# VectorE's background work dealt out by one count in a decoder layer, and down weights loaded later

## The chip, the cores and the metric

The kernel runs on one core of a Trainium2 chip. The metric is the device time of one execution in microseconds (us), median of several runs. The engines are called PE (TensorE, matmuls; its weight loads run beside it as PEld), DVE (VectorE), ACT (ScalarE), POOL (GpSimd) and SP (SyncE, which issues the DMAs).

## The reference

One decoder layer on `x` (2 batches x 512 tokens x 1024), with a LayerNorm behind each of three blocks. Cut to what matters:

```python
q, k, v = x @ wq.T, x @ wk.T, x @ wv.T             # 32 heads of q, 8 of k and v, of 128
s = where(0 <= i - j < 128, q @ k.T / sqrt(128), -inf)   # 4 heads of q share one of k and v
x = layernorm(x + (softmax(s) @ v) @ wo.T)
fq = lambda t: (clip(round(t / s + z), 0, 255) - z) * s  # 8-bit fake quantisation
x = layernorm(x + fq(x) @ fq(ctx))                 # ctx: 1024 x 1024 for each batch
h = x / 128
act = int8(trunc(clip(silu(h @ w_gate.T) * (h @ w_up.T) * 128, -128, 127)))   # 2752 wide
x = layernorm(x + int8(trunc(clip(act @ w_down.T * 128, -128, 127))))
```

The ternary weights `w_gate`, `w_up` and `w_down` come as float32.

## The kernel before

The large products of the attention (projections of q, k and v, and the output product) and of gate and up run in float32 by Strassen's scheme in Winograd's form: a product of two by two blocks is made of seven products of blocks, which PE does as matmuls of 128 x 128 by 128 x 256, and of sums of blocks before and behind, which DVE does. `strassen_right_steps` makes the four sums `t` of the tokens' side (L102 to L108, each over 1024 values a partition), `strassen_left` the four sums `s` of the weights' side (L118 to L121, 512 values), and `strassen` the seven products and the sums of their results (`st`, `vT`, `kT`, `qT`, L147 to L178).

**Attention.** There are 16 groups `m`, (batch b, key head g), each of four token tiles i. While a group's scores, softmax and products with v are worked on (`scores`, `weigh`), `pieces(m + 1)` runs the three projections of the next group ahead, one of 21 steps at a time, and then `transpose_v` (tile `vtr`, L308). At the fifth step (k == 4) of a projection, `prepare` makes the sums L118 to L121 of a later one. The two batches have right sums of their own: `t_1` of batch 1 is made when group 7 of batch 0 starts (m + 1 == NKV, L437).

**Work behind, beside and ahead.** The function `other` is called six times in a tile, 24 times in a group. Each call takes one step of `rest` (the pieces), one step of `keeping` and then calls `between`, which is `in_attention` (L1062). That function has three queues of generators, and takes one step of each `behind` and `aside` in every call, and one of `ahead` in every fourth call or so.
- `keeping` (`keep`, `left_sums`, L405 to L426): the result of two tiles is copied into `factors` (L400), DVE makes the left sums of the output product (L407 to L412: four of 256 values, and behind the second pair of tiles four of 896), and DMAs store them in DRAM as `kept`.
- `behind`: from batch 0, group 2 on, the quantised context (L607 to L617) and the output product of each batch, `project_out`: 56 products `y` (L555) from `ol` (loaded from `kept`, L476) and `or` (loaded `wo` and its sums, L483; sums `ot`, L495 to L500), each set of whose results `read` adds to the residual (L523 to L546). After `read` come `gap` bare yields: four for batch 0, two for batch 1.
- `aside`: `cross_tokens(0)`, the token tiles 2, 3, 0, 1 of batch 0 for the cross product, when `ahead` is empty: LayerNorm (L77 to L85), quantisation (L607 to L617), transposes `q` (L671) copied to `a1T` (L672), product `m` (L678), sums and LayerNorm (L679 to L680, L62 to L85), transposes `x2` (L687) copied to `x2T` (L688), and in the last group the right sums `t2_0` for the feed-forward.
- `ahead`: the sums of the weights of the output product and of gate and up (L1033 to L1036, L1055 to L1058), stored by DMA.

**Feed-forward.** `feed_forward` works through units (batch b, a slice of 128 of the 2752). For each unit it loads the down weights `wd` (`load_down`, L738) and then the next unit's `wgu` and `sgu` (L703 to L706). ACT and DVE split `wd` into `hi` (L757) and `lo` (L758) for the product `d` (L801). `wd` has one buffer.

Within a block of the program a scheduler sets the order of each engine's instructions, from the order in the program and from buffers; the queues above decide where a step stands in the program.

Of the kernel before, what the change touches and what calls it, by code (L numbers as in the profile page):

```python
# [19 lines left out]
B = 2  # L20
# [67 lines left out]
def strassen_right(nc, pool, x, name):  # L88


    steps = strassen_right_steps(nc, pool, x, name)
    for factors in steps:
        pass
    return factors


def strassen_right_steps(nc, pool, x, name):

    b11, b12, b21, b22 = (x[:, ts(k, KH), ts(n, NH)] for k in range(2) for n in range(2))
    t = pool.tile([P, 4, KH, NH], F32, tag="t", name=name)  # L100
    t1, t2, t3, t4 = (t[:, k] for k in range(4))
    nc.vector.tensor_tensor(t1, b12, b11, ALU.subtract)  # L102
    yield
    nc.vector.tensor_tensor(t2, b22, t1, ALU.subtract)
    yield
    nc.vector.tensor_tensor(t3, b22, b12, ALU.subtract)
    yield
    nc.vector.tensor_tensor(t4, b21, t2, ALU.subtract)  # L108
    yield b11, b21, b22, t4, t1, t2, t3


def strassen_left(nc, tc, pool, w, name):
# [66 lines left out]
    yield  # L179


class Background:


    def __init__(self):
# [6 lines left out]
    def step(self):  # L192
        while self.queue:
            item = self.queue[0]
            item[2] += 1
            if item[2] % item[1]:
                return
            try:
                next(item[0])
                return  # L200
            except StopIteration:
                self.queue.pop(0)

# [4 lines left out]


def attention(nc, tc, consts, xbuf, tpool, wpool, ps_p, ps_y, dram, kept, complete, between):  # L210

# [3 lines left out]
    with ExitStack() as ctx:  # L217
# [65 lines left out]
        def project(n):  # L283

            b, g, j = order[n]
            if j == 0:
                c1 = kT[b, g] = kvpool.tile([P, N], F32, tag="kT", name=f"kT_{n}")
                c2 = vT[b, g] = kvpool.tile([P, N], F32, tag="vT", name=f"vT_{n}", bufs=1)
            else:
                if j == 1:  # L290
                    qT[b, g] = qpool.tile([P, N // BLOCK, G, BLOCK], F32, tag="qT", name=f"qT_{b}_{g}")
                c1, c2 = (qT[b, g][:, :, 2 * j - 2 + h] for h in range(2))
            if n == 0:
                project_first((c1, c2))
                yield
                return
            outs = [c[:, ts(half, c.shape[1] // 2)] for c in (c1, c2) for half in range(2)]
            for k, _ in enumerate(strassen(nc, (ps_p, ps_y if b == 0 else ps_p), work, lefts.pop(n), right[b], outs, n)):
                if k == 4:
                    prepare(n + 1)  # L300
                elif k == 6:
                    load_weight(n + 2)
                yield

        def transpose_v(b, g):
            ps = ps_t.tile([P, TPB, P], F32, tag="t", name=f"vtr_{b}_{g}")
# [77 lines left out]
        def weigh(pending, meanwhile):  # L384


            if pending is None:
                meanwhile()
                return
            b, g, i, s = pending  # L390
            cur, both = transpose_p(b, g, i, s)
            meanwhile()
            ps = ps_t.tile([P, G, P], F32, tag="t", name=f"o_{b}_{g}_{i}")
            if i == 0:
                nc.tensor.matmul(ps, v[b, g][:, 0, :], cur, start=True, stop=True)  # L395
            else:
                nc.tensor.matmul(ps, v[b, g][:, i - 1, :], both, start=True, stop=False)  # L397
                nc.tensor.matmul(ps, vd[b, g][:, i - 1, :], cur, start=False, stop=True)  # L398
            half, place = divmod(i, 2)
            nc.scalar.copy(factors[:, 2 * half : 2 * half + 2, 2 * place : 2 * place + 2],  # L400
                           ps.rearrange("p (k j) t -> p k j t", k=2))
            if place:
                keeping.add(keep(b, g, half))
# [10 lines left out]
        def keep(b, g, half):  # L414


            own = slice(2 * half, 2 * half + 2)
            yield from left_sums(*(factors[:, own, k] for k in range(7)))
            yield
            if half:  # L420
                yield from left_sums(*(factors[:, k] for k in range(7)), True)
            for k in (3, 4, 5, 2, 6) if half else (0, 1):
                nc.sync.dma_start(out=kept[b][:, g, k], in_=factors[:, k])
            if half:
                complete.add((b, g, "kept"))
            yield  # L426
# [2 lines left out]

        for _ in pieces(0):  # L430
            pass
        pending = None
        for m, (b, g) in enumerate(groups):
            if m + 2 == NKV:
                x1 = load_x(1)
            if m + 1 == NKV:
                right[1] = strassen_right(nc, tpool, x1, "t_1")  # L437
            rest = pieces(m + 1) if m + 1 < len(groups) else iter(())
            for i in range(TPB):

                def other():
                    next(rest, None)
                    keeping.step()
                    between(b, g, i)

                s = scores(b, g, i, other)
                weigh(pending, other)
                pending = b, g, i, s
                for _ in range(STEPS - 2):
                    other()  # L450
            for _ in rest:
                pass
        weigh(pending, lambda: between(B - 1, NKV - 1, TPB))
        keeping.drain()


def project_out(nc, tc, b, xres, spaces, psum, kept, complete, wo_d, sums, x_d, gap):
# [90 lines left out]
    for n, (k, g) in enumerate(steps):  # L548
        while n + 2 < len(steps) and (b, steps[n + 2][1], "kept") not in complete:
            yield  # L550
        left, mine, sums_now = lefts.pop(n), factors.pop(n), following
        for part in (order[:4], order[4:]):
            for j in part:
                bank, half = places[j]
                nc.tensor.matmul(  # L555
                    banks[bank][:, half], left[:, SLOT[j]], mine[j],
                    start=grow[k][0] and g == 0 and half == 0, stop=g == LAST, skip_group_check=True,
                )
            if part[0] == order[0]:
                next(sums_now, None)  # L560
                yield
        following = right_sums(n + 1)
        next(following)
        load_right(n + 3)
        load_left(n + 2)
        yield
        if g == LAST:
            read(k)
            if k in (5, 3):
                complete.add((b, 1 if k == 5 else 0))  # L570
            for _ in range(gap):
                yield


class Cross:
# [134 lines left out]
def feed_forward(nc, tc, ident, xres, spill, x2T, xbuf, tpool, wpool, left, right, gate_up, wd_d, pools, stream, ps_y, out, between, finish_between):  # L710

    one_pool, raw_pool, b_work, ps_p = pools
    with ExitStack() as ctx:
# [176 lines left out]

        todo, since, ends, room_x = [], [], [], []
        for u, (b, m) in enumerate(units):
            load_down(u)
            load_unit(u + 1)
            if m == NCHUNK:
                if b == 0:
                    finish_between()
                    right[1] = strassen_right(nc, tpool, x2T[1], "t2_1")
                rest_unit(u, b)
            else:  # L900
                g, up = gate_up_tiles(u)
                outs = g[:, :NH], g[:, NH:], up[:, :NH], up[:, NH:]
                for k, _ in enumerate(strassen(nc, (ps_p, ps_y if b else ps_p), work, left.pop(u), right[b], outs, u)):
                    if k == (0 if m == 0 else 3):
                        for args in todo:
                            down(*args)
                        todo = []
                    between(k)
                    if k in (2, 5) and ends:
                        norm(*finish(*ends.pop(0)))  # L910
                activate(u, g, up)
            split(u)
            since.append(u)
            if u < held_from and (len(since) == (4 if b else 2) or u + 1 == held_from):
                assert not todo
                todo = [(since, i, e) for i in range(TPB) for e in range(2)]
                since = []
# [25 lines left out]
def decoder_layer(ctx, tc, x, xT, ctx_kv, wq, wk, wv, wo, s1, z1, s2, z2, wgu, wgu_rest, wd, out):  # L943
# [50 lines left out]
    wo_sums = scratch.tile([P, 4, NKV, 2, HALF], F32, tag="wo_sums", name="wo_sums")  # L994

    def output(b):
        return project_out(nc, tc, b, xres, (resid, stream), ps_y, kept[b], complete, wo, wo_sums, x, 2 if b else 4)

    def cross_tokens(b):
        while ahead.queue:  # L1000
# [4 lines left out]
        while b == 0 and not last_group[0]:  # L1005
            yield
        if b == 0:
            for factors in strassen_right_steps(nc, tpool, x2T[0], "t2_0"):
                yield
            right[0] = factors  # L1010

    def weights_room(n, names):

# [45 lines left out]
            nc.sync.dma_start(out=sums[m][:, 0:3, k : k + 2], in_=s)  # L1059
            nc.sync.dma_start(out=sums[m][:, 3, k : k + 2], in_=a21)  # L1060

    def in_attention(b, g, i):  # L1062
        calls[0] += 1
        place = calls[0] % 6
        if (b, g, i, place) == (0, 2, 0, 1):
# [3 lines left out]
        if (b, g, i, place) == (1, 0, 1, 1):  # L1069
            behind.add(output(0))  # L1070
            behind.add(output(1))
            aside.add(cross_tokens(0))
        behind.step()
        aside.step()
        if b and g == NKV - 1:
            last_group[0] = True
            if place == 0:
                prepare_feed_forward()
        if (place == 0 and (b or g or i)) or (place == 3 and i % 2):
            ahead.step()  # L1080

    left, right = {}, {}

# [3 lines left out]
            if u not in left:  # L1087
                left[u] = load_factors(nc, wpool, gate_up, u, u)

    calls, in_first, last_group = [0], [True], [False]  # L1090
    ahead.add(sum_output_weights())
    ahead.add(sum_weights())
    attention(nc, tc, (ident, mask_i, keep_cur), xbuf, tpool, wpool, pools[3], ps_y,
# [66 lines left out]
```

## Time and profile before

| what | us |
|---|---|
| median of 3 runs (1948.54, 1948.76, 1952.91) | 1948.76 |
| the profiled execution | 1950.62 |
| its span | 1948.9 |
| PE busy | 1891.6 (97%) |
| DVE busy | 1368.4 (70%) |
| ACT busy | 564.3 (29%) |
| PE waits for `vT` (L175) ahead of `vtr` | 13.4, 4 times |
| PE waits for `ol` ahead of `y` | 5.5, 3 times |

The span is the time from the first to the last instruction in the profile. A matmul of 128 x 256 in float32 takes 0.38 us by the profile, and the pitch from one to the next is 0.43 us. A busy share is an average over all stages; what a change is worth is read in the place where an engine waits. The mean clock granted to PE over the span was 0.99 of full speed, and it falls in a few short stretches to half.

### The profile page before, as it was taken

What the parts mean: (1) busy time and instruction counts of PE and PEld (TensorE: products, weight loads), DVE (VectorE), ACT (ScalarE), POOL (GpSimd) and SP (SyncE); (2) the same over time, 40 slices, a digit from 0 to 9 for tenths busy, and PEclk for the clock granted to TensorE, in tenths of its full rate; (3) what the DMA queues carried; (4) which work ended last, traced back from release to release, by engine and by line L of the source; (5) the groups of instructions that cost most, each with busy time, mean ns of one, the idle gap of its engine ahead of it and who ended that gap; (6) DMA issues with size and microseconds to landing.
All of it is one profiled execution on the core that took longest, in us unless ns stands there. A gap on an engine that the chain in (4) does not pass through costs nothing.

```text
span 1948.9 us, 24631 instructions
## 1 busy us (share of the span) xinstructions
PE 1891.6 (97%) x8658; PEld 1553.0 (80%) x8668; DVE 1368.4 (70%) x3010; ACT 564.3 (29%) x1571; POOL 13.7 (1%) x32
## 2 busy tenths in 40 slices
PE   9999999999999999999899999999999999999997
PEld 6888888878888888888676788888877778888885
DVE  4678888777667677767776776566768697554656
ACT  1333343323122221233433221111233255221224
POOL 0000000000000000000000000000000000000000
PEclk9999999999999999999899999999999999999999
DMA  8478787767698788764376765666653245543421
GB/s 302 158 269 286 271 288 265 257 240 265 228 312 296 249 299 285 231 220 170 126 275 226 246 226 203 208 219 219 219 189 119 82 155 196 184 167 124 147 92 43
DMA packets 183323, 416.87 MB, mean 214 GB/s; under 512 B 16672, under 2 KB 93728, under 8 KB 183200
## 3 DMA queue, kind: packets, MB, share of 16 engines
q1 hardware_dynamic: 181760, 412.94, 61.7%
q10 hardware_dynamic: 1440, 2.36, 0.3%
q8 instruction: 68, 1.11, 0.2%
q14 instruction: 55, 0.45, 0.1%
HBM read 318.77 MB, written 96.47 MB: 213 GB/s over the span
## 4 chain that ended last, share of the span: by engine, by line
PE 77%; DVE 12%; DMA 6%; ACT 3%; issue 2%; SPq 0%; DVEq 0%; ACTq 0%
PE prod L138 43%; PE y L555 14%; PE d L801 7%; DMA wd<-in_wd_dram 4%; PE ps L338 3%; PE o L397 2%; PE o L398 2%; PE m L678 1%; PE pt L374 1%; ACT s L362 1%; PE first L273 1%; PE o L395 1%; DVE lo L758 1%; DVE factors L408 1%; DMA sums<-sum 1%
## 5 line engine op out<-in xcount | busy, mean ns | idle before, releaser
L555 PE MATMUL y<-or,ol 128*128 128x256 f32 x896 | 248.8, 382 | 5.6 <-DMA ol<-kept 5.5
L555 PEld LDWEIGHTS y<-or,ol 128*128 128x128 f32 x896 | 169.7, 191 | 31.8 <-issue 4.8
L555 PE MATMUL y<-ot,ol 128*128 128x256 f32 x672 | 184.4, 383 | 3.9 <-DVE ot L496 2.6
L138 PE MATMUL prod<-xT,w 128*128 128x256 f32 x752 | 184.0, 382 | 0.0
L138 PE MATMUL prod<-t,w 128*128 128x256 f32 x752 | 177.7, 379 | 0.0
L138 PE MATMUL prod<-t,s 128*128 128x256 f32 x752 | 177.2, 380 | 0.5 <-ACT kT L158 0.5
L138 PE MATMUL prod<-x2T,wgu 128*128 128x256 f32 x672 | 161.0, 380 | 1.7 <-ACT st L147 1.7
L138 PEld LDWEIGHTS prod<-xT,w 128*128 128x128 f32 x752 | 140.2, 191 | 27.6 <-issue 10.6
L138 PEld LDWEIGHTS prod<-t,w 128*128 128x128 f32 x752 | 140.2, 190 | 24.4 <-issue 7.2
L138 PEld LDWEIGHTS prod<-t,s 128*128 128x128 f32 x752 | 140.0, 190 | 24.6 <-issue 5.7
L138 PE MATMUL prod<-t,wgu 128*128 128x256 f32 x672 | 157.4, 380 | 1.8 <-DVE st L150 1.6
L138 PE MATMUL prod<-t,sgu 128*128 128x256 f32 x672 | 157.2, 380 | 1.5 <-ACT u L795 0.8
L555 PEld LDWEIGHTS y<-ot,ol 128*128 128x128 f32 x672 | 126.0, 191 | 27.1 <-DVE ot L496 8.2
L138 PEld LDWEIGHTS prod<-x2T,wgu 128*128 128x128 f32 x672 | 127.6, 191 | 20.9 <-ACT st L147 2.5
L138 PEld LDWEIGHTS prod<-t,wgu 128*128 128x128 f32 x672 | 127.1, 190 | 21.1 <-DVE st L150 2.4
L138 PEld LDWEIGHTS prod<-t,sgu 128*128 128x128 f32 x672 | 126.9, 190 | 20.7 <-ACT x2T L688 1.6
L348 ACT COPY s<-ps 128x128 f32<-128x128 f32 x192 | 39.7, 233 | 246.6 <-PE ps L338 246.6
L362 ACT ACTIVATE s<-s,top 128x128 f32<-128x128 f32 x256 | 100.2, 393 | 33.0 <-DVE top L359 32.6
L801 PE MATMUL d<-hi,act 128*128 128x512 f32 x256 | 108.4, 424 | 0.9 <-DVE act L781 0.4
L801 PE MATMUL d<-lo,act 128*128 128x512 f32 x256 | 101.5, 397 | 0.0
L815 DVE TENSOR_TENSOR acc<-d,acc 128x512 f32<-128x512 f32 x104 | 71.4, 690 | 41.4 <-PE d L801 40.9
L161 DVE TENSOR_TENSOR st<-prod,st 128x256 f32<-128x256 f32 x89 | 37.6, 422 | 89.3 <-PE prod L138 89.2
(213 smaller groups left out, 3000.1 us busy)
## 6 DMA issues: line engine op xcount, KB each, us to landing
kept<-factors SPq DMA_DIRECT2D x112, 448.0 KB, 3.8
ol<-kept SPq DMA_DIRECT2D x112, 448.0 KB, 5.0
w<-in_wq_dram SPq DMA_DIRECT2D x64, 512.0 KB, 4.5
or<-wo_sums SPq DMA_DIRECT2D x64, 512.0 KB, 4.7
sgu<-sums SPq DMA_DIRECT2D x42, 768.0 KB, 5.7
or<-in_wo_dram SPq DMA_DIRECT2D x48, 512.0 KB, 4.7
wgu<-in_wgu_dram SPq DMA_DIRECT2D x42, 512.0 KB, 4.0
wd<-in_wd_dram SPq DMA_DIRECT2D x42, 512.0 KB, 4.5
```

Source lines behind the costliest of these rows:

```text
L138: nc.tensor.matmul(ps, left[k - 1][:, c, :], right[k - 1][:, c, :], start=start and c == 0, stop=c == KH - 1, skip_group_check=True)
L161: nc.vector.tensor_tensor(u3, two, p1, ALU.add)
L273: nc.tensor.matmul(ps[h][:, part], weights[0][:, h, c], x0[:, c, part], start=c == 0 and k == 0, stop=c == KC - 1, skip_group_check=True,)
L338: nc.tensor.matmul(ps[:, k, cut // BLOCK : G + 1].rearrange("p d w -> p (d w)"), qT[b, g][:, G * i + c].rearrange("p h w -> p (h w)"), kT[ ...
L348: nc.scalar.copy(s[:, c, c * BLOCK :], ps[:, k, : G - c].rearrange("p d w -> p (d w)"))
L362: nc.scalar.activation(s[:, h, :], s[:, h, :], AF.Exp, bias=top[:, h : h + 1], scale=QSCALE, accum_out=total[:, h : h + 1],)
L374: nc.tensor.transpose(ps[:, :, ts(c, BLOCK)], s[:, c, :], ident)
L397: nc.tensor.matmul(ps, v[b, g][:, i - 1, :], both, start=True, stop=False)
L398: nc.tensor.matmul(ps, vd[b, g][:, i - 1, :], cur, start=False, stop=True)
L555: nc.tensor.matmul(banks[bank][:, half], left[:, SLOT[j]], mine[j], start=grow[k][0] and g == 0 and half == 0, stop=g == LAST, skip_group_ ...
L801: nc.tensor.matmul(ps, act[:, ts(i, P)], half[:, ts(e, HALF)], start=start and k == 0, stop=stop and k == len(parts) - 1)
L815: nc.vector.tensor_tensor(acc[t][:, ts(e, HALF)], ps, acc[t][:, ts(e, HALF)], ALU.add)
```

## The change

`strassen_right_steps` gives back its result and four functions, one for each sum. For `t_1` the first two are called when the group starts, and each of the next calls of `other` makes one more. One count replaces the fixed places of the queues: each call of `in_attention` steps `behind`; if the call already had a large step (k == 4 of a projection, a right sum, or a `read` that is followed by `gap`) nothing more is done; else one step of `keeping`, if it has any; else, with a credit of four calls, one step of `ahead`; else one of `aside`. `keeping` is emptied before `factors` is written again, and a bare yield in `keep` stays only for the second half. `gap` is two for both batches. In the feed-forward the next unit's gate and up weights are loaded first, and the unit's down weights after its second product. The diff, cut to that:

```diff
 def strassen_right_steps(nc, pool, x, name):
...
-    nc.vector.tensor_tensor(t1, b12, b11, ALU.subtract)
-    yield
...
+    less = lambda *which: lambda: nc.vector.tensor_tensor(*which, ALU.subtract)
+    return (b11, b21, b22, t4, t1, t2, t3), (less(t1, b12, b11), less(t2, b22, t1), less(t3, b22, b12), less(t4, b21, t2))
...
+LUMP = "lump"
...
 class Background:
             try:
-                next(item[0])
-                return
+                return next(item[0])
...
 def attention(...):
                     prepare(n + 1)
...
-                yield
+                yield LUMP if k == 4 else None
...
+            keeping.drain()
             nc.scalar.copy(factors[...], ps.rearrange(...))
...
             yield from left_sums(*(factors[:, own, k] for k in range(7)))
-            yield
             if half:
+                yield
                 yield from left_sums(*(factors[:, k] for k in range(7)), True)
...
             if m + 1 == NKV:
-                right[1] = strassen_right(nc, tpool, x1, "t_1")
+                right[1], late = strassen_right_steps(nc, tpool, x1, "t_1")
+                late = list(late)
+                for _ in range(2):
+                    late.pop(0)()
...
                 def other():
-                    next(rest, None)
-                    keeping.step()
-                    between(b, g, i)
+                    lump = next(rest, None)
+                    if late:
+                        late.pop(0)()
+                        lump = LUMP
+                    between(b, g, i, lump, keeping)
...
 def project_out(...):
-            for _ in range(gap):
-                yield
+            for j in range(gap):
+                yield None if j else LUMP
...
 def feed_forward(...):
         for u, (b, m) in enumerate(units):
-            load_down(u)
             load_unit(u + 1)
+            if m == NCHUNK:
+                load_down(u)
...
+                    if k == 1:
+                        load_down(u)
                     between(k)
...
-        return project_out(..., 2 if b else 4)
+        return project_out(..., 2)
...
-            for factors in strassen_right_steps(nc, tpool, x2T[0], "t2_0"):
+            right[0], steps = strassen_right_steps(nc, tpool, x2T[0], "t2_0")
+            for step in steps:
+                step()
                 yield
...
-    def in_attention(b, g, i):
+    def in_attention(b, g, i, lump, keeping):
         calls[0] += 1
         place = calls[0] % 6
...
-        behind.step()
-        aside.step()
+        if behind.step():
+            lump = LUMP
+
+        credit[0] += 1
+        if lump:
+            pass
+        elif keeping.queue:
+            keeping.step()
+        elif credit[0] >= 4 and ahead.queue:
+            credit[0] -= 4
+            ahead.step()
+        else:
+            aside.step()
...
-        if (place == 0 and (b or g or i)) or (place == 3 and i % 2):
-            ahead.step()
```

More of the change, by code (lines that the diff above doesn't have):

```diff
@@ L88, in strassen_right @@
 def strassen_right(nc, pool, x, name):
-    steps = strassen_right_steps(nc, pool, x, name)
-    for factors in steps:
-        pass
+    factors, steps = strassen_right_steps(nc, pool, x, name)
+    for step in steps:
+        step()
     return factors
@@ L101, in strassen_right_steps @@
     t1, t2, t3, t4 = (t[:, k] for k in range(4))
-    nc.vector.tensor_tensor(t1, b12, b11, ALU.subtract)
-    yield
-    nc.vector.tensor_tensor(t2, b22, t1, ALU.subtract)
-    yield
-    nc.vector.tensor_tensor(t3, b22, b12, ALU.subtract)
-    yield
-    nc.vector.tensor_tensor(t4, b21, t2, ALU.subtract)
-    yield b11, b21, b22, t4, t1, t2, t3
+    less = lambda *which: lambda: nc.vector.tensor_tensor(*which, ALU.subtract)
+    return (b11, b21, b22, t4, t1, t2, t3), (less(t1, b12, b11), less(t2, b22, t1), less(t3, b22, b12), less(t4, b21, t2))
 def strassen_left(nc, tc, pool, w, name):
@@ L418, in keep @@
             yield from left_sums(*(factors[:, own, k] for k in range(7)))
-            yield
             if half:
+                yield
                 yield from left_sums(*(factors[:, k] for k in range(7)), True)
@@ L431, in attention @@
             pass
-        pending = None
+        pending, late = None, []
         for m, (b, g) in enumerate(groups):
@@ L452, in attention @@
                 pass
-        weigh(pending, lambda: between(B - 1, NKV - 1, TPB))
+        weigh(pending, lambda: between(B - 1, NKV - 1, TPB, None, keeping))
         keeping.drain()
@@ L570, in project_out @@
                 complete.add((b, 1 if k == 5 else 0))
-            for _ in range(gap):
-                yield
+            for j in range(gap):
+                yield None if j else LUMP
 class Cross:
@@ L996, in output @@
     def output(b):
-        return project_out(nc, tc, b, xres, (resid, stream), ps_y, kept[b], complete, wo, wo_sums, x, 2 if b else 4)
+        return project_out(nc, tc, b, xres, (resid, stream), ps_y, kept[b], complete, wo, wo_sums, x, 2)
     def cross_tokens(b):
@@ L1007, in cross_tokens @@
         if b == 0:
-            for factors in strassen_right_steps(nc, tpool, x2T[0], "t2_0"):
+            right[0], steps = strassen_right_steps(nc, tpool, x2T[0], "t2_0")
+            for step in steps:
+                step()
                 yield
-            right[0] = factors
     def weights_room(n, names):
@@ L1088, in prepare_feed_forward @@
                 left[u] = load_factors(nc, wpool, gate_up, u, u)
-    calls, in_first, last_group = [0], [True], [False]
+    calls, credit, in_first, last_group = [0], [0], [True], [False]
     ahead.add(sum_output_weights())
```

## The prediction

> **What bounds the kernel now.** I read the page first: who is busy, then the clock.
>
> ```profile
> PE 1891.6 (97%) x8658; PEld 1553.0 (80%) x8668; DVE 1368.4 (70%) x3010; ACT 564.3 (29%) x1571; POOL 13.7 (1%) x32
> ...
> PEclk9999999999999999999899999999999999999999
> ```
>
> TensorE (PE) is the bound: 1891.6 of 1948.9 us, and the change removes no matmul. It can only win what PE loses: 57.3 us of idle time, and half of any time in which PE runs at half clock. The single 8 in the clock line says that such time exists. The waits of PE, totalled, say what it idles for (columns: us in total, times, longest):
>
> ```profile
> PE vtr L308 <- DVE vT L175: 13.4, 4, 7.5
> PE y L555 <- DMA ol<-kept: 5.5, 3, 2.7
> ...
> PE pt L374 <- DVE s L368: 1.2, 1, 1.2
> ```
>
> The largest is the transpose of v (`vtr`) waiting for VectorE's (DVE's) last sum of v. The third view is a table of windows around the long waits (us; busy PE, PEld, DVE, ACT, POOL; granted clock; DMA share; GB/s):
>
> ```profile
> 392.00:418.00 26.00, 21.30 (x88) 16.30 (x87) 20.82 (x45) 8.09 (x32) 0.00 (x0) 0.87 0.69 242
> 940.00:960.00 20.00, 11.17 (x45) 6.65 (x45) 13.96 (x28) 6.52 (x20) 0.00 (x0) 0.66 0.46 168
> 1008.00:1045.00 37.00, 32.11 (x128) 23.10 (x127) 21.66 (x54) 12.17 (x51) 0.00 (x0) 0.91 0.58 210
> 1045.00:1080.00 35.00, 29.26 (x124) 23.52 (x124) 29.76 (x59) 10.56 (x14) 0.00 (x0) 0.97 0.88 317
> 1080.00:1430.00 350.00, 347.70 (x1578) 292.65 (x1579) 230.53 (x469) 61.34 (x97) 0.00 (x0) 1.00 0.63 217
> ```
>
> A window's loss is its length less PE's busy time, plus its length times (1 − clock). A, 392 to 418: 4.7 + 3.4 = 8.1 us. C, 940 to 960: 8.8 + 6.8 = 15.6. D1, 1008 to 1045: 4.9 + 3.3 = 8.2. D2, 1045 to 1080: 5.7 + 1.1 = 6.8. Together 38.7 us in 118 us; the 350 us behind them lose 2.3. So the change is decided in four places.
>
> **Place A: the two sums of `t_1` and what follows.** VectorE in order of time:
>
> ```profile
> 403.44 1.08 DVE L407 TENSOR_TENSOR factors<-factors 128x896 f32<-128x896 f32 x1
> 404.44 0.69 DVE L118 TENSOR_TENSOR s<-w 128x512 f32<-128x512 f32 x1
> 405.04 1.08 DVE L408 TENSOR_TENSOR factors<-factors 128x896 f32<-128x896 f32 x1
> ...
> 407.85 1.09 DVE L411 TENSOR_TENSOR factors<-factors 128x896 f32<-128x896 f32 x1
> 408.85 1.09 DVE L412 TENSOR_TENSOR factors<-factors 128x896 f32<-128x896 f32 x1
> 409.85 0.42 DVE L175 TENSOR_TENSOR vT<-prod,st 128x256 f32<-128x256 f32 x1
> ```
>
> Starts lie about 1.0 us apart for a big sum and 0.6 for a sum of the next weights (L118 to L121), so 4 x 1.0 + 4 x 0.6 = 6.4 us stand between the previous sum of v and L175. PE waits 4.24 us behind it. In the changed order, which a build shows without a run, L411 and L412 stand behind L175: 2.0 us leave, and the wait is 2.2 at most. The group's four sums of 1.22 us (L102 to L108) are now spread over 8 us of PE work, the last of them 2 us later than before, with three weight sums of 0.42 (L1056 to L1058) between and four fewer behind; adding rows in that order leaves a wait of 0.7 us. I take 0.7 to 2.2 and no half clock, since waits of 1.2 (462 us) and 1.9 us (1146 us) stand in the trace with none behind them. A then loses 0.7 to 2.2 instead of 8.1: saved 5.9 to 7.4, taken 6.7. If the clock still trips, 2.5.
>
> **Place C: batch 1, group 6.** The same transpose waits longest here:
>
> ```profile
> 949.71 0.87 PE L308 MATMUL vtr<-ident,vT 128*128 128x128 f32 x3 [7.53 <-DVE vT L175]
> ...
> 954.17 2.34 PE L678 MATMUL m<-a,a1T 128*128 128x512 bf16 x5 [1.30 <-ACT s L362]
> ```
>
> Between the sums of v at 938.41 and 949.13 VectorE takes three small and four big left sums, the four L118s and the LN and quantise steps of one token tile (L85 0.82, L607 0.82, L612 and L613 0.70 each): 10.7 us in a row, of which PE covers three. In the changed order the quantise steps are elsewhere, the next weights' four stand behind the transposes, and three big sums, 3.1 us, remain, of which the product between (4 matmuls, 0.43 us apart) covers 1.7. So 1 to 2.5 us remain, no half clock. The moved token steps need their own place; the nearest rows, PE's wait of 1.30 for L362 above and 0.3 to 0.7 for L679 and the like, give 2 us more. C loses 3 to 4.5 instead of 15.6: saved 11.1 to 12.6, taken 11. Floor: if the 2.0 us that A loses are all that goes, PE still waits 5.5 + 1.3 and the clock trips: saved 2.
>
> **Place D1: the last group.** Something is given back here. Background work is rationed: a step that carries a lump, or that has kept sums queued, leaves nothing for `aside` (the token tiles). So tile 1's LN, quantise and products move from group 6 into group 7, among tiles 2 and 3. Adding rows in the changed order from the mask multiply of group 6's last tile (L380) to tile 1's second LN (L85): 8 left sums 5.5, LN and quantise 8.3, the softmax pieces L352 to L368 4.9, two L380 1.2, other 0.8: 20.7 us of VectorE beside 15.2 of PE. So PE stands 5.5 us behind by the transposes of x2. In front of it the first `m` follows its transposes directly, with no other product between, so it waits for the copies L672, 2 x 1.0 plus a hand-over: 2.2 to 2.95, taken 2.6. With `o` behind `both` (1.46, its row in D1), `q` 0.7, `act` 1.2: 11.5 us. Before, PE lost 4.9 here and ran 6.8 us at half clock (3.3). With a like spell of half clock, 2.5: 14.0 us after against 8.2, so 5.8 us given back. Bounds: none of the VectorE backlog reaches PE: 6 + 0, a gain of 2; PE at half clock in proportion to C (6.8 lost on 8.8 idle): 11.5 + 8.9 = 20.4, 12 given back.
>
> [...]
>
> **Place D2: `ol` behind `wd`.** At 1075.44 and 1078.19 PE waits 2.69 and 0.88 us for `ol`, whose loads leave SP's queue at 1069.30 and 1072.34, around the loads of `wd` (1060.52 and 1072.99) and a unit's own loads; the DMA share is 0.88. The change puts `wd` two products later in its unit, here behind `ol`. What then comes late is `d` behind `act` (0.78 at most in the trace) and `lo` (L758, 1.22 us) behind the `wd` landing, 1.6 to 2.5. D2 saves 4.3 to 5.2 of 6.8; 1 if the two waits are for room in the ring. Taken 5.
>
> **The rest.** The order of PE's products is the same from unit 3 to unit 21. In units 24 to 32 one split stands a place later: the row "PE prod L138 <- DVE u L164", 4.3 us in five waits, may gain or lose 1. `output(0)`'s shorter gap lets each of its steps begin two calls earlier: the additions hide under PE where DVE is 70% busy; a wait more like "PE y L555 <- DVE ot L496", 2.6 us in two, costs 1.3. Smaller waits for L352 in batch 0: 0.7. I charge 2 in all. Instructions added or removed: none; only two of four `t_1` sums, the tokens and loads move.
>
> **Sum.** 6.7 + 11 − 5.8 + 5 − 2 = 14.9 us. The profiled execution took 1950.62 (span 1948.9 and 1.7 around it), 1.9 above the median of 1948.76. So 1950.6 − 14.9 = 1935.7 for that one and 1933.9 for the median; I say 1934.
>
> **Rivals.** *Slower (1957): the last group stays at half clock.* If D1's waits follow one another so closely that the clock does not return over the 28 us of PE work from tile 1's `q` to the end of attention, each of these us takes two: 28 lost, + 11.5, against 8.2: 31.3 given back, where A, C and D2 save 22.7: 1948.8 + 8.6 + 2 = 1959; at 90% of it 1956. It turns the sign from 29 us lost in D1 on, and is told from no change from 35 on. For it: the clock of 0.91 after waits of 1.2 us. Against: one 20-us window, with 8.8 us idle, still had 0.66.
> *Waits shrink, the clock trips all the same (1943).* A saves 2.5, C 5 (a wait of 4 us left with its trip of 6.8), D1 gives back 5.8, D2 saves 5, 2 for the rest: 4.7 to 6 gained, 1943 to 1944. For it: `t_1` still shares VectorE's queue with kept sums.
> *The order moves but the same items end last (1947 to 1950).* If `ol` waits for room and the waits of A and C become waits for other lumps of the same size, nothing is left but noise: 0 ± 2. Against: 2.0 us leave A's queue and 6 leave C's by the order itself.
> *D1 is free (1927).* PE's other work, output products of batch 1, absorbs the backlog: − 5.8 becomes + 1.
>
> **How the numbers follow.** Forecast (1928 to 1942) 0.53; free D1 (1925 to 1928) 0.12; clock trips (1942 to 1946) 0.17; no change 0.07; half clock throughout 0.11. No difference under 0.3%, 5.8 us, can be told from none: faster is below 1942.9, slower above 1954.6. Faster: 0.53 + 0.12 + 0.13 of the third = 0.78; same: 0.04 + 0.07 + 0.01 = 0.12; slower: the other 0.10. A range of 1925 to 1948 leaves out the last case and small ends.
>
> **What would show it.** Right: no `vtr` behind L175 above 2.5 us, clock 0.97 or more over 392 to 418 and 1.00 over 930 to 960; more waits of `m`, `pt`, `ps` and `x2` between 1000 and 1040; no `y` behind `ol` above 1 us near 1075. Wrong: a clock under 0.8 over the last group, or vT waiting behind `t_1`.

## The result and the profile after

The changed kernel takes 1932.49 us (median of four runs, 1928.50 to 1933.06), the kernel before 1950.72 beside it; the ratio is 0.9902, 95% interval 0.9882 to 0.9922. The forecast was 1934, 0.8% less than before; 1.0% less is what came. The profiled execution took 1932.87 with a span of 1931.1, 17.8 us shorter than before. A line of the kernel before has another number now: L138 is L132, L175 is L169, L407 to L412 are L406 to L411, L118 to L121 are L112 to L115, L496 and L500 are L501 and L505, L555 is L560, L672 is L677, L678 is L683, L687 is L692, L801 is L806.

The page of the changed kernel, engine totals and clock:

```profile
PE 1886.3 (98%) x8668; PEld 1550.9 (80%) x8668; DVE 1367.3 (71%) x3010; ACT 563.0 (29%) x1571; POOL 13.7 (1%) x32
...
PEclk9999999999999999999989999999999999999999
```

The same work of VectorE, 1 us less, lies elsewhere; PE's idle time fell from 57.3 to 44.8 us. The 8 in the clock line has moved one slice on, from C to the last group. PE's waits, totalled:

```profile
PE prod L132 <- DVE u L158: 6.4, 6, 1.8
PE y L560 <- DVE ot L501: 4.9, 6, 2.1
...
PE ps L336 <- DVE s L350: 2.8, 2, 2.6
...
PE m L683 <- ACT a1T L677: 1.6, 2, 1.4
...
PE x L692 <- DVE xres L85: 1.5, 1, 1.5
...
PE vtr L306 <- DVE vT L169: 1.3, 1, 1.3
```

`vtr` behind `vT` fell from 13.4 us to 1.3, and `y` behind `ol` (5.5) is gone from the list. New are `ps` and `x`, and `m` rose from 0.2; all three stand among tile 1's steps in the last group. Windows of equal length cut the two executions at different work, since the second runs ahead; so the stretches are cut here where PE has the same amount of work behind it. The kernel before, stretches A, C, D1, D2 (start:end, length, then busy PE, PEld, DVE, ACT, POOL, granted clock, DMA share, GB/s):

```profile
387.70:430.50 42.80, 38.07 (x169) 30.13 (x168) 32.29 (x70) 12.22 (x49) 0.00 (x0) 0.92 0.69 237
929.30:966.90 37.60, 28.77 (x127) 21.24 (x127) 28.10 (x68) 15.69 (x44) 0.00 (x0) 0.82 0.36 128
991.00:1047.90 56.90, 51.62 (x223) 38.60 (x222) 39.54 (x90) 22.61 (x83) 0.00 (x0) 0.94 0.67 245
1047.90:1108.80 60.90, 55.16 (x237) 44.59 (x236) 45.24 (x90) 15.40 (x20) 0.00 (x0) 0.97 0.76 267
```

The changed kernel, the same four:

```profile
387.00:423.90 36.90, 35.49 (x168) 28.55 (x168) 31.95 (x70) 12.22 (x49) 0.00 (x0) 1.00 0.78 263
923.80:948.50 24.70, 24.66 (x126) 19.73 (x126) 19.36 (x47) 17.04 (x45) 0.00 (x0) 1.00 0.42 158
973.20:1034.50 61.30, 53.43 (x233) 39.14 (x232) 45.65 (x103) 25.99 (x82) 0.00 (x0) 0.92 0.67 246
1034.50:1088.80 54.30, 52.30 (x236) 43.78 (x235) 42.61 (x86) 15.16 (x20) 0.00 (x0) 1.00 0.79 282
```

The second column is the verdict of each place: A 42.8 to 36.9, 5.9 saved; C 37.6 to 24.7, 12.9 saved, with PE idle for 0.04 us; D1 56.9 to 61.3, 4.4 given back; D2 60.9 to 54.3, 6.6 saved. The stretch between A and C is 1.1 longer, and the rest gives 2.1 back: 5.9 + 12.9 − 4.4 + 6.6 − 1.1 − 2.1 = 17.8.

VectorE in the changed kernel in place A shows the queue that the prediction described:

```profile
401.54 1.08 DVE L406 TENSOR_TENSOR factors<-factors 128x896 f32<-128x896 f32 x1
...
405.35 0.68 DVE L115 TENSOR_TENSOR s<-w,s 128x512 f32<-128x512 f32 x1
405.95 0.41 DVE L169 TENSOR_TENSOR vT<-prod,st 128x256 f32<-128x256 f32 x1
406.29 1.08 DVE L410 TENSOR_TENSOR factors<-factors 128x896 f32<-128x896 f32 x1
407.29 1.08 DVE L411 TENSOR_TENSOR factors<-factors 128x896 f32<-128x896 f32 x1
```

From 401.54 to 405.95 are 4.4 us instead of 6.4, and the two big sums L410 and L411 now come behind the sum of v.

### The profile page after: what moved, and what is told of

Read it like the earlier page. It is cut to its first block, busy times and chain, and to the rows that moved or that the text cites. A ratio compares the mean times of both kernels' runs of the same rounds, so it can differ in the third digit from the quotient of the medians.

```text
span 1931.1 us, 24627 instructions
## 1 busy us (share of the span) xinstructions
PE 1886.3 (98%) x8668; PEld 1550.9 (80%) x8668; DVE 1367.3 (71%) x3010; ACT 563.0 (29%) x1571; POOL 13.7 (1%) x32
## 4 chain that ended last, share of the span: by engine, by line
PE 44%; DVE 8%; DMA 6%; ACT 3%; issue 1%; SPq 0%; DVEq 0%; ACTq 0%
PE prod L132 23%; PE y L560 10%; PE d L806 6%; DMA wd<-in_wd_dram 4%; DVE lo L763 1%; PE m L683 1%; DMA raw<-in_ctx_dram 1%; ACT hi L762 1%; PE ps L336 1%; PE o L395 1%; PE o L396 1%; DMA or<-in_wo_dram 0%; PE x L692 0%; DVE halves L763 0%; PE d_last L806 0%
## 5 line engine op out<-in xcount | busy, mean ns | idle before, releaser
L560 PE MATMUL y<-or,ol 128*128 128x256 f32 x896 | 246.8, 380 | 0.0
L560 PE MATMUL y<-ot,ol 128*128 128x256 f32 x672 | 184.4, 383 | 5.5 <-DVE ot L501 4.9
L560 PEld LDWEIGHTS y<-or,ol 128*128 128x128 f32 x896 | 169.0, 190 | 24.3 <-issue 1.4
L132 PE MATMUL prod<-xT,w 128*128 128x256 f32 x752 | 184.2, 381 | 0.2
L132 PE MATMUL prod<-t,w 128*128 128x256 f32 x752 | 177.2, 379 | 0.0
L132 PE MATMUL prod<-t,s 128*128 128x256 f32 x752 | 177.1, 379 | 0.1
L132 PE MATMUL prod<-x2T,wgu 128*128 128x256 f32 x672 | 162.6, 382 | 2.0 <-ACT st L141 2.0
L132 PEld LDWEIGHTS prod<-xT,w 128*128 128x128 f32 x752 | 139.6, 190 | 26.9 <-issue 9.6
L132 PE MATMUL prod<-t,wgu 128*128 128x256 f32 x672 | 158.6, 382 | 1.3 <-DVE st L144 1.3
L132 PEld LDWEIGHTS prod<-t,w 128*128 128x128 f32 x752 | 140.1, 190 | 24.3 <-issue 7.7
L132 PEld LDWEIGHTS prod<-t,s 128*128 128x128 f32 x752 | 140.3, 190 | 23.7 <-issue 5.3
L132 PE MATMUL prod<-t,sgu 128*128 128x256 f32 x672 | 156.9, 380 | 0.8 <-ACT x2T L693 0.8
L560 PEld LDWEIGHTS y<-ot,ol 128*128 128x128 f32 x672 | 125.2, 190 | 30.3 <-DVE ot L501 11.6
L132 PEld LDWEIGHTS prod<-x2T,wgu 128*128 128x128 f32 x672 | 128.3, 191 | 21.4 <-ACT st L141 2.8
L132 PEld LDWEIGHTS prod<-t,wgu 128*128 128x128 f32 x672 | 128.3, 192 | 20.8 <-DVE st L144 2.1
L132 PEld LDWEIGHTS prod<-t,sgu 128*128 128x128 f32 x672 | 127.0, 190 | 19.5 <-ACT x2T L693 1.6
L806 PE MATMUL d<-hi,act 128*128 128x512 f32 x256 | 108.6, 424 | 2.2 <-DMA or<-in_wo_dram 1.5
L806 PE MATMUL d<-lo,act 128*128 128x512 f32 x256 | 101.5, 397 | 0.0
```

What stands on the lines that cost most here:

```text
L132: nc.tensor.matmul(ps, left[k - 1][:, c, :], right[k - 1][:, c, :], start=start and c == 0, stop=c == KH - 1, skip_group_check=True)
L560: nc.tensor.matmul(banks[bank][:, half], left[:, SLOT[j]], mine[j], start=grow[k][0] and g == 0 and half == 0, stop=g == LAST, skip_group_ ...
L806: nc.tensor.matmul(ps, act[:, ts(i, P)], half[:, ts(e, HALF)], start=start and k == 0, stop=stop and k == len(parts) - 1)
```

## The experiments

The first five take the change apart: two parts alone, the one count alone, the change without one part, and one size of it undone.

**t_1 dealt out, alone.**

```diff
-                right[1] = strassen_right(nc, tpool, x1, "t_1")
+                right[1], late = strassen_right_steps(nc, tpool, x1, "t_1")
+                late = list(late)
+                for _ in range(2):
+                    late.pop(0)()
...
+                    if late:
+                        late.pop(0)()
```

> The kernel before, with the four sums of t_1 dealt out (two at the group's start, one in each of the next two calls) and nothing else changed. Theory 1 (the prediction's: A's wait went because L411 and L412 moved behind L175, which the one count does, not this part): the 6.4 us of left sums and next weights' sums stay ahead of L175, so PE still waits 3.5 to 4.2 us for vT near 406 us, the clock still trips, and the time is 1948 to 1950. Theory 2 (spreading the sums is what cures A): the wait falls below 2 us, the clock stays at 1.00 from 392 to 418 us, and the time falls by 6 to 7 us to about 1943. C, D1 and D2 as before in both.

Measured: 1949.94, ratio 0.9998 (0.9985 to 1.0012). PE's wait for vT in A is 3.32 us instead of 4.24, and half clock follows it (0.93 over 392 to 418 us). That is just under the 3.5 us of theory 1 and far from theory 2: the spread is worth 0.9 us of idle time, which no time shows.

**The down weights loaded later, alone.**

```diff
-            load_down(u)
             load_unit(u + 1)
...
+                    if k == 1:
+                        load_down(u)
```

> The kernel before, with only the down weights loaded later in a unit. Theory 1: the waits of y for ol near 1075 us (2.7 and 0.9) go, D2 loses 2 instead of 6.8, the time is about 1944. Theory 2: the waits for ol stay, since the loads of ol are held by something else than wd; the time stays at 1948 to 1950, with the split of wd (L757, L758) some 0 to 2 us better or worse in the units from 16 on.

Measured: 1948.98, ratio 0.9988 (0.9977 to 1.0000). PE in D2:

```profile
1070.55 1.10 PE L555 MATMUL y<-or,ol 128*128 128x256 f32 x4 [1.08 <-DMA ol<-kept]
1073.58 0.77 PE L801 MATMUL d<-hi,act 128*128 128x512 f32 x1 [1.92 <-issue]
```

The wait for `ol` shrinks from 2.69 to 1.08, the other of 0.88 goes, and `d`, which waited 0.31, waits 1.92: 3.9 us became 3.0. The time is theory 2's, but not its reason: the waits for `ol` did shrink, and most of what they lost came back as a wait of `d`, for which the profile shows no releaser.

**The one count alone** (with the two gap yields and the freed yield in `keep`; `t_1` at once, down weights early).

```diff
-                right[1], late = strassen_right_steps(nc, tpool, x1, "t_1")
...
+                right[1] = strassen_right(nc, tpool, x1, "t_1")
...
+            load_down(u)
             load_unit(u + 1)
...
-                    if k == 1:
-                        load_down(u)
```

> The changed kernel, with t_1's four sums at the group's start again and the down weights loaded where they were before: the one count and the two gap yields alone. Theory 1 (the prediction's: D2 was saved by the later down weights): A 2 to 3 us idle and perhaps no half clock, C as in the changed kernel, but y waits again 3 to 5 us for ol between 1040 and 1080 us: 1937 to 1939. Theory 2 (the count moves the second output product as well, and that is what freed ol): no wait of y for ol, 1932 to 1934, the same as the changed kernel.

Measured: 1933.06, ratio 0.9908 (0.9889 to 0.9926): the whole gain. No `y` waits for `ol`, with the down weights loaded as before the change. PE's list has instead:

```profile
PE vtr L306 <- DVE vT L169: 2.2, 1, 2.2
...
PE m L680 <- ACT s L348: 1.7, 1, 1.7
...
PE x L689 <- DVE xres L85: 1.6, 1, 1.6
```

A's wait is 2.2, the upper end that the prediction gave, and half clock follows it for 3.4 us, which the prediction had left out. Theory 2: the prediction's cause for D2 falls.

**t_1 at once in the changed kernel** (down weights late).

```diff
-                right[1], late = strassen_right_steps(nc, tpool, x1, "t_1")
...
+                right[1] = strassen_right(nc, tpool, x1, "t_1")
```

> The changed kernel, with t_1's four sums at the group's start again and the down weights loaded late. Theory 1 (the spread of t_1 is worth 0.9 us of idle time in A, with the count as without it, and the late down weights nothing): PE waits 2.2 us for vT near 405 us, with 0 to 3.4 us of half clock: 1932.5 to 1935. Theory 2 (split and late loads only show together): over 1936 or under 1931.

Measured: 1932.11, ratio 0.9918 (0.9903 to 0.9932), with 2.24 us behind vT in A, then half clock for 3.4 us (0.93 over 392 to 418). Theory 1: 0.9 us again, as without the count.

**Four gap yields for batch 0.**

```diff
-        return project_out(..., 2)
+        return project_out(..., 2 if b else 4)
```

> The changed kernel, with four bare yields behind a read of batch 0's output product again. Theory 1 (the gap only decides how soon a read's sums meet others): the waits of y for ot in batch 0 (five, 2.8 us) shrink by 1 to 2, the time is 1931 to 1933. Theory 2 (the gap sets when the token tiles become ready, and with four both tile 0 and tile 1 fall into the last group, where no projections are left to fill PE): D1 loses 5 to 10 us more than the 11.3 of the changed kernel, the time is 1937 to 1942.

Measured: 1936.34 (1932.31 to 1938.05), ratio 0.9921 (0.9904 to 0.9937), an interval that overlaps the changed kernel's; the trace tells what the time doesn't. PE's waits:

```profile
PE x L692 <- DVE xres L85: 9.9, 3, 7.3
```

From 985 to 1045 PE is idle for 12.0 us at a clock of 0.88; in the changed kernel for 6.3 at 0.91. Against that D2 is idle for 1.0 instead of 2.0. The trace follows theory 2, the gap decides which group the token tiles fall into; its time (1937 to 1942) isn't reached, and the profiled execution, the fastest of the four, earned the price back.

**The token tiles in every call again.**

```diff
+        aside.step()
         if lump:
             pass
...
-        else:
-            aside.step()
```

> The changed kernel, with one step of the token tiles (aside) in every call again, while the left sums (keeping) still give way to lumps. Theory 1 (C was saved because the tokens' LN and quantise steps no longer meet the left sums): C's waits come back in part, 5 to 9 us idle between 930 and 985 us with 3 to 7 us lost at half clock, D1 loses 8 to 11 (about as now), A stays below 2 us idle: 1941 to 1948. Theory 2 (the left sums alone did it): C stays free, the last group gains 3 us since tile 1 comes earlier: 1929 to 1932.

Measured: 1945.33, ratio 0.9980 (0.9971 to 0.9990). PE between 940 and 952 us:

```profile
945.21 1.99 PE L132 MATMUL prod<-t,w 128*128 128x256 f32 x8 [0.59 <-DVE st L155]
...
951.49 0.61 PE L676 MATMUL q<-ident_bf,a 128*128 128x128 bf16 x8 [2.56 <-DVE vT L169]
```

From 930 to 985 PE is idle for 5.8 us, at a clock of 1.00; from 985 to 1045 for 9.4. A keeps its 1.32. Theory 1, but without half clock in C; 3.5 us of idle time between 800 and 930, where the changed kernel has 0.1, were not foreseen, nor was D2, where `y` waits 1.29 us for `ol` again and PE is idle for 3.9 us at a clock of 0.90.

**The left sums in every call again.**

```diff
+        keeping.step()
         if lump:
             pass
-        elif keeping.queue:
-            keeping.step()
```

> The changed kernel, with one step of the left sums (keeping) in every call again, while the token tiles still give way. Theory 1 (A was saved by the left sums giving way to the next weights' sums; C by both): A waits 3 to 4 us for vT again and loses 1.7 to 3.4 more at half clock, C waits 3 to 6 with 2 to 7 at half clock, the last group gains 3 since the tokens come earlier: 1938 to 1946. Theory 2 (the spread of t_1 and the tokens' giving way are enough): 1932 to 1934, the same as the changed kernel.

Measured: 1947.46, ratio 0.9989 (0.9979 to 0.9999). VectorE in A:

```profile
407.55 0.69 DVE L115 TENSOR_TENSOR s<-w,s 128x512 f32<-128x512 f32 x1
408.15 1.09 DVE L410 TENSOR_TENSOR factors<-factors 128x896 f32<-128x896 f32 x1
409.15 1.09 DVE L411 TENSOR_TENSOR factors<-factors 128x896 f32<-128x896 f32 x1
410.15 0.42 DVE L169 TENSOR_TENSOR vT<-prod,st 128x256 f32<-128x256 f32 x1
```

L410 and L411 are ahead of the sum of v again, PE waits 4.66 us (put down to the row behind the sum of v), and half clock lasts 6.8 (0.87 over 392 to 418); from 930 to 985 PE is idle for 5.3. Theory 1, and 1.5 us dearer than its range: D2's waits are back as well (5.4 idle). So neither queue may run free here: with only one of them held back, 2 or 4 of the 18 us are left by the ratios. Part of that loss is D2's in both kernels.

**Tile 1's steps earlier.**

```diff
         elif keeping.queue:
             keeping.step()
+            if b and g == NKV - 2 and i >= 1:
+                aside.step()
```

> The changed kernel, with one step of the token tiles also in the calls that take a step of the left sums, in batch 1's group 6 from the second tile on, and nowhere else: tile 1's steps move back from the last group into group 6, but not into its lumps. Theory 1 (D1's loss is tile 1's chain in a group that has no projections to fill PE): the stretch 985 to 1045 loses 5 to 7 us instead of 11, the waits of ps for s and of x for xres go, D2 loses 2 us more, since the second output product moves too: 1928 to 1931. Theory 2 (the chain costs the same wherever it stands): C takes what D1 loses: 1932 to 1934.

Measured: 1930.05, ratio 0.9910 (0.9892 to 0.9928). Tile 1 moved only part of the way: its last transposes of x2 start 19 us behind the last product of a projection, 27 in the changed kernel and 1.5 before. From 985 to 1045 PE loses 5.0 idle + 3.6 at half clock, 8.6 instead of 6.3 + 5.4; D2 loses 3.8 + 1.8 instead of 2.0. The time is theory 1's, but D1 saves less than it said (5 to 7 left), the waits of `ps` and `x` shrink to 0.7 and 1.0 and don't go, and D2 gives back more. Run again beside the changed kernel on one chip:

> The kernel with tile 1's steps back in group 6, beside the changed kernel on the same chip. Theory 1 (tile 1's chain costs less where projections fill PE, less the wait for ol that comes back): 1 to 4 us below the changed kernel. Theory 2 (what it saves in the last group, the returned waits for ol take): within 1 us of it.

Measured: 1928.02 against 1929.03, for which 1930 to 1934 had been expected (ratios to the kernel before 0.9885, 0.9865 to 0.9904, and 0.9892, 0.9873 to 0.9911). PE in D2 of this kernel:

```profile
1050.28 1.10 PE L560 MATMUL y<-or,ol 128*128 128x256 f32 x4 [1.05 <-DMA ol<-kept]
1053.34 0.76 PE L806 MATMUL d<-hi,act 128*128 128x512 f32 x1 [1.96 <-issue]
```

At 1.0 us apart, with intervals that overlap, the time doesn't decide between the two. The trace has what theory 2 says: D1's loss shrinks, but D2's waits return. That fits the other kernels so far. By the same distance, `y` waits for `ol` for 1 us or more near D2 wherever tile 1 ends early (before, `t_1` dealt out and `wd` late alone: 1.5 us; the free queues: −32 and −6; this one: 19), and in none where it ends late (the changed kernel 27, the count alone and `t_1` at once 26, four yields 43), wherever `wd` is loaded.

**A faster version.** The same, with three gap yields for batch 1's output product and weight sums at a credit of three in batch 1:

```diff
-        return project_out(..., 2)
+        return project_out(..., 3 if b else 2)
...
-        elif credit[0] >= 4 and ahead.queue:
+        elif credit[0] >= 4 - b and ahead.queue:
```

> The same with three gap yields for batch 1's output product and the weight sums stepped at a credit of three calls in batch 1, so that its reads and token tiles end at other places of the units: adding rows in its order, 2 to 3 us less idle time of PE in the units 15 to 22 (now 4.9 between 1430 and 1580 us) and 1 us less in batch 1's attention: 2 to 4 us below the kernel with tile 1 back in group 6, 1925 to 1929. Rival: small waits change places but not their sum: no difference.

Measured: 1919.53 (1918.95 to 1925.00), ratio 0.9850 (0.9828 to 0.9872), 9.5 us below the changed kernel on the same chip and well past the forecast. Its stretches from the last group on:

```profile
985.00:1090.00 105.00, 97.24 (x426) 78.03 (x427) 78.81 (x165) 31.79 (x73) 0.00 (x0) 0.98 0.76 277
1090.00:1430.00 340.00, 338.92 (x1553) 287.09 (x1552) 228.55 (x477) 63.32 (x104) 0.00 (x0) 1.00 0.61 213
1430.00:1580.00 150.00, 146.51 (x668) 114.32 (x667) 122.26 (x239) 58.90 (x87) 1.93 (x3) 1.00 0.37 130
```

PE is idle for 7.8, 1.1 and 3.5 us; the changed kernel, profiled beside it, for 9.5, 2.7 and 4.6. Though tile 1 ends 19 us behind the last projection here too, neither `ol` nor `d` keeps PE waiting in D2. It waits there for `st` (1.13) and `ot` (1.41) instead and is idle for 3.6 us from 1045 to 1080, against 4.3 with tile 1 earlier alone and 1.8 in the changed kernel; from 985 to 1090 its clock is 0.98, where tile 1 earlier alone has 0.97. Cut at equal work, its execution gains 3.4 us up to the end of D2, 1.1 to unit 5, and some 4 in the units 14 to 20, and loses 1 in the last units: 7.3 us of span. Without the credit:

```diff
-        elif credit[0] >= 4 - b and ahead.queue:
+        elif credit[0] >= 4 and ahead.queue:
```

> The combined version without the credit of three calls: tile 1's steps back in group 6 and three gap yields for batch 1's output product. Theory 1 (the third yield does it: after the first units the reads of the second output product stand elsewhere, and `or` and `ol` are in time): ratio to the kernel before about 0.986, within 2 us of the combined version. Theory 2 (the earlier weight sums do it): ratio about 0.9885, as with tile 1's steps alone.

Measured: 1922.49, ratio 0.9868 (0.9848 to 0.9888). By the medians, each against the kernel before beside it, it lies nearer to the combined version (0.9857; 0.9844 and 0.9887 for tile 1's steps alone); by the ratios with their intervals it lies in the middle, and its interval overlaps both. Its trace has the combined version's D2, with no wait for `ol` or `d`, and its span is 1920.1 us, against 1917.6 and 1926.2. So the third yield frees `ol` and does most in the profiled executions; the credit's share stays open.

## Why the prediction was right

Its sum was 14.9 us against 17.8 in the profiled execution. Term by term:

- **Place A, 6.7:** 5.9, the lower end of its range. The step held to its detail: 2.0 us leave the queue, 1.31 us of wait remain (0.7 to 2.2 forecast), and the count alone leaves 2.2, the end worked out without the spread. The wait of 1.22 at 462 us, which the sum left out, is gone too. That 2.2 us would bring no half clock was wrong, and the spread kept it from counting.
- **Place C, 11:** 12.9. The cause holds: with either queue free, PE is idle for 5.3 or 5.8 us from 930 to 985, against 1.7 in the changed kernel and 8.9 before. Mis-sized was the leftover, 3 to 4.5 us; PE was idle for 0.04, since VectorE's three big sums lie fully beside products, and the moved token steps cost nothing before the last group. That a wait of up to 2.5 us there would bring no half clock was the author's estimate; with 0.04 us left this run did not test it.
- **Place D1, −5.8:** −4.4. The mechanism and its waits are there, smaller: the backlog of VectorE was put at 5.5 us, and its two waits measure 2.56 (`ps`) and 1.51 (`x`), with 0.22 ahead; `m` behind `a1T` 1.43 instead of 2.6; `o` behind `both` 1.45 for 1.46. A wait of 1.98 for `ol` (at 1017.81) was part of the 4.9 us that the prediction read there before; its sum left that wait out without saying so, and it is gone. These are tile 1's steps in the last group, PE of the changed kernel:

```profile
984.60 1.90 PE L683 MATMUL m<-a,a1T 128*128 128x512 bf16 x8 [1.43 <-ACT a1T L677]
...
993.12 1.44 PE L336 MATMUL ps<-kT,qT 128*128 128x160 f32 x4 [2.56 <-DVE s L350]
...
998.41 1.97 PE L692 MATMUL x<-ident,xres 128*128 128x128 f32 x8 [1.51 <-DVE xres L85]
```

  The half clock there was forecast at 2.5; the stretch's 0.92 is 4.9, and 1.7 in another execution of the same kernel.
- **Place D2, 5:** 6.6, but this step failed in its cause. The prediction gave the saving to `wd` being loaded behind `ol`. The late load alone saves 0.9 us of idle time there, and the count without it has the full saving. SP's queue shows what stood ahead of `ol` instead, before and in the changed kernel:

```profile
1064.30 0.33 SPq L627 DMA_DIRECT2D raw<-in_ctx_dram  x1
1068.92 0.33 SPq L483 DMA_DIRECT2D or<-in_wo_dram  x1
1069.30 0.42 SPq L476 DMA_DIRECT2D ol<-kept  x1
```

```profile
1048.06 0.33 SPq L632 DMA_DIRECT2D raw<-in_ctx_dram  x1
1048.43 0.43 SPq L481 DMA_DIRECT2D ol<-kept  x1
1053.35 2.29 SPq L488 DMA_DIRECT2D or<-in_wo_dram  x2
```

  Before, the load of `ol` stands behind a load of `or` that waits 4.2 us for VectorE's sums of a `read` (`xres`, L527). In the changed kernel it stands ahead of that load, and so it does in the count alone and with `t_1` at once. In each of the kernels with up to two yields and a wait for `ol` in D2, the order is the one before. With two yields, this goes with tile 1's place: D1's loss and D2's saving are two ends of one shift, and with tile 1 earlier both shrink. The third yield frees `ol` as well. No run moved the load of `or` alone, so this cause is read from the traces and not tested.
- **The rest, −2:** −3.2. The waits of `y` for `ot` rose from 3.5 us in three to 4.9 in six, five of the six in batch 0's output product, where the prediction counted one place more. Those of `prod` for `u` rose from 4.3 to 6.4, twice the 1 that it allowed; in another execution they are 3.8.

The terms miss by −0.8, 1.9, 1.4, 1.6 and −1.2, 2.9 in all, so the size isn't a product of large errors that cancel. But that D2's 5 stood near 6.6 was luck, since the cause given for it is worth 0.9. The slower rival did not come about: D1 lost 7.9 idle and 4.9 at half clock, against the 29 that it needed. The rival in which the clock trips all the same came about in A only in the two kernels with the count and without the spread of `t_1`, for 3.4 us, which is a loss of 1.7.

## What to carry to other kernels

Where one engine is full and another, at 70%, feeds it in order, look in the second one's queue for long instructions that stand between a result and its only reader: moving two of 1 us behind it cut PE's wait from 4.2 to 2.2 us here. Where several background queues share that engine, hold them all back by one count: with one of the two free, nearly the whole gain was lost here. And read a part's worth by running it alone: two parts were worth nothing measurable, and one saving had been put down to one of them.

## What the runs showed of the hardware

The granted clock fell to half in a few spells. In the kernel before it was 0.50 for 6.83 us in A (408.85 to 415.68), 13.65 in C (944.75 to 958.40), 6.82 in D1 (1036.91 to 1043.73) and 3.41 in D2 (1077.87 to 1081.28); in the changed kernel for 10.25 us in D1 (992.70 to 1002.95) and 3.40 from 1129.30 on; and in both at the end, from 1941.44 and 1924.60 on. The kernel with the count alone, three stretches of 3.41 us around its 2.2 us wait in A:

```profile
404.19:407.60 3.41, 1.18 (x9) 0.86 (x7) 3.41 (x6) 0.59 (x1) 0.00 (x0) 1.00 0.81 229
407.60:411.01 3.41, 3.41 (x9) 2.22 (x8) 3.19 (x7) 0.58 (x1) 0.00 (x0) 0.50 1.02 408
411.01:414.42 3.41, 3.41 (x18) 2.99 (x17) 1.89 (x6) 1.78 (x7) 0.00 (x0) 1.00 0.64 254
```

In the first PE is busy for 1.18 us and the clock is 1.00, in the second it is busy throughout at 0.50, with 9 matmul records instead of 18, in the third it is back at 1.00. (A `prod` of four float32 matmuls of 128 x 256 stands in the trace as eight records, 0.22 us apart at a clock of 1.00.)

The length of a wait alone does not tell whether half clock comes. A wait of 1.3 us in A left the clock at 1.00 from 392 to 418 us in four kernels (the changed one, four gap yields, the token tiles in every call, tile 1's steps earlier); one of 2.2 went with 0.93 there in both that had it (the count alone, `t_1` at once). A wait of 2.08 us of `y` for `ot` in the changed kernel, up to 1128.22 us, was followed by the 3.40 us at 0.50; one of 1.92 in the kernel before, up to 1148.01, was not (1.00 from 1143 to 1160). The same wait of 7.5 us in C went with 13.65 us at 0.50 in the kernel before and with 6.86 where `t_1` alone was dealt out. And 2.56 us in the kernel with the token tiles free left the clock at 1.00 from 930 to 985. What else decides was not shown.
